# Taps 0 to 3 of a convolution on four 64x64 tiles of TensorE in place of two 64x128 tiles

## The chip, the cores and the metric

The kernel runs on one core of one Trainium2 chip. The metric is the device time of one execution in microseconds (us). Before the change it is 3138.06 us, the median of 3 runs that lie between 3136.07 and 3140.17 us.

## The reference, cut to what matters

Three layers of the same form (layers 0 to 2) and then a fourth of another kind work on `x`, 4 images of 32x32 positions with 16 channels, all in float32. The change touches only the first three:

```python
first = jnp.einsum('ijpq,bpqc->bijc', M2, inputs)
K = jnp.transpose(G, (2, 3, 4, 0, 1, 5)).reshape(kh, kw, c, h * w * f)
shifted = lax.conv_general_dilated(inputs, K, window_strides=(1, 1), padding='SAME',
                                   dimension_numbers=('NHWC', 'HWIO', 'NHWC'))
shifted = shifted.reshape(b, h, w, h, w, f)
diff = jax.nn.relu(inputs[:, :, :, None, None, :] - shifted)
second = jnp.einsum('ijpq,bpqijc->bijc', W2, diff)
return first - L * second
...
x = x + _L0_conv_ref(_gn(x), L0_conv_M, L0_conv_Wp, L0_conv_G)
```

`shifted` is a 3x3 convolution with 1024 x 16 = 16384 output channels: each position (i, j) has filters of its own, and each of them is run over the whole image. `second` then weighs the 1024 image positions for every (i, j) and adds them up. `_gn` is a group norm. The fourth layer is a filter with an infinite impulse response, done in the reference through FFTs; the kernel does it as products with a Toeplitz matrix.

## The kernel before, in words

The 16384 output channels of a layer are cut into 128 blocks of 128 (8 positions by 16 channels). One block for one of the 4 images is called a **group** here; three layers have 3 x 128 x 4 = 1536 groups, and they make up nearly all of the work.

In a group (`conv_layer`, lines 464 to 486) TensorE computes the convolution of the block for all 1024 positions into a PSUM tile `pt` of 128 partitions by 2 by 512. The two `half`s are the upper and lower 16 image rows. Half 0 takes its operands from SBUF partitions 0 to 63 and half 1 from 64 to 127, so that the two are on different row tiles of the array, each 64 rows by 128 columns, and run side by side. Nine taps of 16 channels are 144 rows of contraction, which are split in three steps `n`:

- n = 0: `ga`, taps 0 to 3 of the reordered list (line 41), 64 rows, float32
- n = 1: `gb`, the next four taps, 64 rows, float32
- n = 2: `gn`, the ninth tap, 64 rows in float32r. Its 16 channels stand there four times: the rounded weights and the remainders, against the high and low parts of the image.

A float32 product appears in the trace as two pairs of a weight load (LDWEIGHTS) and a product (MATMUL), a float32r product as one pair. So the 3072 calls with `ga` (1536 groups, two halves) are 6144 records, and the 3072 calls with `gn` are 3072.

`prepare_g` (line 386) subtracts the identity from the centre tap in `ga`, so that `pt` holds `shifted - inputs`. VectorE then does min(pt, 0) times W and adds up along the 1024 positions in one instruction (line 478). Its result is the block's part of `- second`.

The order of the work is written out by hand (`manual_schedule`, line 76). PSUM has 4 buffers `pt`; a group's first product waits until VectorE has read the buffer's last contents. After every group, `step()` advances what stands in `todo`, and after every block one step of `beside` runs. These put other TensorE work between two groups: `first_term` (line 324, 128 rows by 64 columns, two column tiles; line 312, transposes on the whole array), the impulse response in layer 0 (lines 523, 566 and 605, shape 64x128, and for the last, shorter block of line 523 shape 64x64), and group sums (line 101). After the last group, line 761 does the fourth layer on four tiles of 128 rows by 32 columns.

Weights come in by DMA on the SP queue: W for two blocks at a time (`load_w`, line 409, 6 buffers), G for eight blocks at a time (`load_g`, line 364; 2 buffers for `ga`, `gb` and `gn`, and one for the ninth tap's source `g9`). `prepare_g` for the next eight blocks runs in the midst of a chunk, partly on ACT (line 402) and VectorE (line 405).

Of the kernel before, what the change touches and what calls it, by code (L numbers as in the profile page):

```python
# [37 lines left out]
P = 128  # L38
B, C, S = 4, 16, 32
# [4 lines left out]
GC = 8  # L44
# [10 lines left out]
def conv_stack_kernel(ctx, tc, x, raw, w0, M, W, G, den, num, h0, cst, dft, one, idp, idq, out):  # L55
    nc = tc.nc
# [13 lines left out]
    def pair_psum():  # L70
        return ps.tile([P, 2, 512], F32, tag="pt", name="pt")
# [292 lines left out]
    def load_g(layer, ch, parts=((slice(0, GC), nc.sync, nc.sync, nc.sync),)):  # L364

        layer, ch = at = chunk(layer, ch)
        if layer == 3 or at in gr:
            return
        gr[at] = ga, gb, g9 = [
            pool.tile([P, GC, P], F32, tag=tag, name=tag) for pool, tag in ((gs, "ga"), (gs, "gb"), (gp, "g9"))  # L370
        ]
        flat = lambda t: t.rearrange("r n m -> r (n m)")
        for part, *queues in parts:
            src = G[layer][:, (ch * GC + part.start) * P : (ch * GC + part.stop) * P]
            for half in range(2):
                rows = slice(64 * half, 64 * half + 64)
                queues[0].dma_start(out=flat(ga[rows, part]), in_=src[:64])
                queues[1].dma_start(out=flat(gb[rows, part]), in_=src[64:P])
            yield
            queues[2].dma_start(  # L380
                out=flat(g9[:, part]),
                in_=src[P : P + C].unsqueeze(0).to_broadcast([8, C, (part.stop - part.start) * P]),
            )
            yield

    def prepare_g(layer, ch, part=slice(0, GC)):


        at = chunk(layer, ch)
        if at[0] == 3 or (part.start == 0 and at in gt):  # L390
            return
        if part.start == 0:
            gt[at] = *gr[at][:2], gs.tile([P, GC, P], F32R, tag="gn", name="gn")
        ga, gb, gn = (t[:, part] for t in gt[at])
        g9 = gr[at][2][:, part]

        gv = ga.rearrange("r n (p f) -> r (n p) f", f=C)
        nc.gpsimd.tensor_tensor(  # L398
            gv, gv, mid.unsqueeze(1).to_broadcast([P, gv.shape[1], C]), ALU.subtract
        )  # L400
        yield
        nc.scalar.copy(gn, g9)  # L402
        for r in (32, 96):
            lo = gn[r : r + 32]
            nc.vector.tensor_tensor(lo, g9[r : r + 32], lo.bitcast(F32), ALU.subtract)  # L405
# [3 lines left out]
    def load_w():  # L409

        layer, at = divmod(len(wts), NBLK // 2)
        if layer == 3:
            return
        cc, q = divmod(2 * at, S)
        wt = wp.tile([P, 2, S * S], F32, tag="w", name="w")
        src = W[layer][cc, :, q : q + 2, :].rearrange("p k m -> p (k m)")
        nc.sync.dma_start(
            out=wt.rearrange("p k m -> p (k m)"),
            in_=src.unsqueeze(1).to_broadcast([8, C, 2 * S * S]) if wts else w0,
        )  # L420
        wts.append(wt)
# [3 lines left out]
    def step():  # L425
        todo[:] = [t for t in todo if next(t, t) is not t]

    def drain():
        while todo:
            step()  # L430

    def conv_layer(layer, xt, finish, side=(), late=iter(())):


        acc = [work.tile([P, 2, NBLK], F32, tag=f"acc{a}", name=f"acc{a}") for a in range(2)]
        xn = xp.tile([P, B, NBLK], F32, tag="x", name="x")
        result = {}

        def beside():
            result["xr"] = yield from first_term(layer, xt)  # L440
            yield from side

        beside = beside()
        last = range(NBLK - GC, NBLK)

        jobs = [(range(GC), (0, 1)), (range(GC), (2, 3))] if layer else [(range(GC), range(B))]
        jobs += [(range(blk, blk + GC), range(B)) for blk in range(GC, NBLK - GC, GC)]
        jobs += [(last, (0, 1)), (last, (2, 3))]
        for job, (blks, batches) in enumerate(jobs):
            pairs = layer and job < 2, job >= len(jobs) - 2  # L450
            for k, blk in enumerate(blks):
                if any(pairs):

                    if k in ((4, 6) if job != len(jobs) - 2 else (0, 2)):
                        load_w()
                elif k % 2 == 0:
                    load_w()
                if k == (3 if job == 0 else 1):
                    list(load_g(layer, blk // GC + 1))
                if (job or not layer) and k == 6:  # L460
                    list(prepare_g(layer, blk // GC + 1))
                if job == len(jobs) - 2:
                    next(late, None)
                wt = wts[64 * layer + blk // 2][:, blk % 2, :]
                for b in batches:
                    pt = pair_psum()
                    for n, (w, im) in enumerate(zip(gt[layer, blk // GC], ims[b // 2])):
                        for half in range(2):
                            rows = slice(64 * half, 64 * half + 64)
                            nc.tensor.matmul(  # L470
                                pt[:, half, :],
                                lhsT=w[rows, blk % GC, :],
                                rhs=im[rows, :, b % 2, :, :S],
                                start=n == 0,
                                stop=n == 2,
                            )
                    junk = junkp.tile([P, S * S], F32, tag="junk", name="junk")
                    nc.vector.scalar_tensor_tensor(  # L478
                        junk,
                        pt.rearrange("p h m -> p (h m)"),  # L480
                        0.0,
                        wt,
                        ALU.min,
                        ALU.mult,
                        accum_out=acc[b // 2][:, b % 2, blk : blk + 1],
                    )
                    step()
                if not any(pairs) and layer + job:
                    next(beside, None)
            if pairs[1]:  # L490
                a = batches[0] // 2
                two = slice(2 * a, 2 * a + 2)
                nc.vector.tensor_tensor(xn[:, two], result["xr"][:, two], acc[a], ALU.add)  # L493
                drain()
                todo.append(finish(a, xn))
                step()
        return xn
# [151 lines left out]
    with tc.tile_pool(name="st", bufs=1) as st:  # L649
        halves = slice(0, 2), slice(2, GC)  # L650
        load_first(0, 0, nc.sync)
        load_first(0, 1, nc.scalar)
        load_first(0, 2, nc.gpsimd)
        loads = load_g(
            0,
            0,
            (
                (halves[0], nc.sync, nc.scalar, nc.gpsimd),
                (halves[1], nc.sync, nc.sync, nc.gpsimd),
            ),  # L660
        )
        next(loads)
        next(loads)
        load_first(1, 0, nc.sync)
        load_first(1, 1, nc.sync)
        load_first(1, 2, nc.gpsimd)
        load_w()
        list(loads)
        first_images()
        load_w()  # L670
        loads = load_g(0, 1)
        next(loads)
        load_w()
        load_w()
        todo.append(loads)
        xs = conv_layer(0, xs, make_image, impulse_response())
    xs = conv_layer(1, xs, make_image)


# [45 lines left out]
    def late_toeplitz():  # L725
# [7 lines left out]
        yield from load_toeplitz(order[TB + 1], *parts)  # L733

    xs = conv_layer(2, xs, norm3, toeplitz(), late_toeplitz())
    drain()

# [15 lines left out]
    for n, k in enumerate(order):  # L753
        if n == 1:
            list(load_toeplitz(order[-1], toeplitz_tile(tp)))
        for slot in slots[k // 2]:
            for cc in range(4):
                for tile, block, q in slot:
# [5 lines left out]
                        lhsT=y3[:, cc, at : at + 8, :].rearrange("p q b -> p (q b)"),  # L764
                        rhs=ts[n][q][:, :, : S - 8 * cc],
                        start=(tile, block) not in every[:done],
                        stop=(tile, block) not in every[done + 1 :],
# [105 lines left out]
```

## Time and profile before

| what | value |
|---|---|
| median of 3 runs | 3138.06 us |
| the profiled execution, whole | 3145.93 us |
| its span, first to last instruction | 3144.1 us |
| granted TensorE clock, mean | 0.997 |
| first and last end of a group | 16.5 us, 3087.0 us |
| line 470, products with `ga`, `gb`, `gn` | 6144, 6144, 3072 records |
| line 470, loads with `ga`, `gb`, `gn` | 188, 186, 186 ns mean |
| line 478 on VectorE | 1536 of 1225 ns, and 1536 of 83 ns to read the sum |

The profile shows one execution. PE is TensorE's products, PEld its weight loads, which overlap the products; DVE is VectorE, ACT ScalarE, POOL GpSimd, and SP the queue that issues most DMAs. A group line reads: line, engine, operation, output and inputs, shape of the array's part used (rows by columns), operand, count, then busy time and mean of one, then the idle time ahead of it and what ended that. The products are pipelined: a record covers the whole way of a product through the array, and the next one's record begins before it has ended. So the distance from one record's start to the next one's is what a product costs, not its length. The chain of waits follows the work that ended last back to the start, step by step, and shows it in order of time.

### The profile page before, as it was taken

What the parts mean: (1) busy time and instruction counts of PE and PEld (TensorE: products, weight loads), DVE (VectorE), ACT (ScalarE), POOL (GpSimd) and SP (SyncE); (2) the same over time, 40 slices, a digit from 0 to 9 for tenths busy, and PEclk for the clock granted to TensorE, in tenths of its full rate; (3) what the DMA queues carried; (4) which work ended last, traced back from release to release, by engine and by line L of the source; (5) the groups of instructions that cost most, each with busy time, mean ns of one, the idle gap of its engine ahead of it and who ended that gap; (6) DMA issues with size and microseconds to landing.
All of it is one profiled execution on the core that took longest, in us unless ns stands there. A gap on an engine that the chain in (4) does not pass through costs nothing.

```text
span 3144.1 us, 39279 instructions
## 1 busy us (share of the span) xinstructions
PE 3113.4 (99%) x16260; PEld 1538.3 (49%) x16260; DVE 2070.0 (66%) x3318; ACT 81.8 (3%) x107; POOL 232.6 (7%) x258
## 2 busy tenths in 40 slices
PE   7999999999999999999999999999999999999998
PEld 3445554445544554444444444455444444444444
DVE  6666766666666766666666666776666666666662
ACT  1000000000000000000000000000000000000000
POOL 1002321000000100100000000010010000000000
PEclk9999999999999999999999999999999999999999
DMA  7554344433343565433333344265544444444411
GB/s 167 150 125 106 83 105 107 104 91 88 87 103 78 121 141 129 98 88 88 97 98 88 87 97 98 69 133 145 126 106 103 96 106 108 101 97 107 111 31 21
DMA packets 67462, 321.20 MB, mean 102 GB/s; under 512 B 10114, under 2 KB 17028, under 8 KB 41812
## 3 DMA queue, kind: packets, MB, share of 16 engines
q1 hardware_dynamic: 56496, 300.10, 40.5%
q10 hardware_dynamic: 6484, 10.81, 1.7%
q0 software_dynamic: 4304, 7.79, 1.3%
q8 instruction: 127, 2.08, 0.3%
q14 instruction: 51, 0.42, 0.1%
HBM read 313.03 MB, written 5.63 MB: 101 GB/s over the span
## 4 chain that ended last, share of the span: by engine, by line
PE 97%; DMA 2%; DVE 1%; issue 0%; SPq 0%; ACT 0%; DVEq 0%
PE pt L470 94%; PE pt L761 1%; DMA g<-in_G_dram 1%; DMA w<-in_W_dram 1%; PE pt L324 1%; DMA im<-in_raw_dram 0%; DVE junk L478 0%; PE pt L523 0%; PE pt L566 0%; PE pt L605 0%; PE pt L101 0%; DVE x L493 0%; DVE s L110 0%; PE pt L312 0%; DVE gn L405 0%
## 5 line engine op out<-in xcount | busy, mean ns | idle before, releaser
L478 DVE SCALAR_TENSOR_TENSOR junk<-pt,w 128x1024 f32<-128x1024 f32 x1536 | 1881.1, 1225 | 996.8 <-PE pt L470 979.9
L470 PE MATMUL pt<-im,ga 64*128 64x512 f32 x6144 | 1587.1, 591 | 7.5 <-DVE junk L478 4.6
L470 PE MATMUL pt<-im,gb 64*128 64x512 f32 x6144 | 1578.2, 589 | 3.2 <-ACT im L179 3.2
L470 PE MATMUL pt<-im,gn 64*128 64x512 f32 x3072 | 1252.3, 806 | 0.0
L470 PEld LDWEIGHTS pt<-im,gb 64*128 64x128 f32 x6144 | 596.1, 186 | 730.6 <-issue 724.2
L470 PEld LDWEIGHTS pt<-im,ga 64*128 64x128 f32 x6144 | 600.3, 188 | 443.4 <-DVE junk L478 286.4
L470 PEld LDWEIGHTS pt<-im,gn 64*128 64x128 f32 x3072 | 299.8, 186 | 361.8 <-issue 360.6
L398 POOL TENSOR_TENSOR ga<-ga,cs 128x1024 f32<-128x1024 f32 (+2 forms) x49 | 113.5, 2316 | 2131.9 <-DMA ga<-in_G_dram 2131.0
L405 DVE TENSOR_TENSOR gn<-g,gn 32x1024 fp32r<-32x1024 f32 (+2 forms) x98 | 120.7, 1231 | 12.4 <-ACT gn L402 10.2
L478 DVE DVE_READ_ACCUMULATOR junk<-pt,w 128x1 f32 x1536 | 128.0, 83 | 0.0
L402 ACT CAST gn<-g 128x1024 fp32r<-128x1024 f32 (+2 forms) x49 | 50.4, 1028 | 2357.7 <-DMA g<-in_G_dram 2133.7
L348 POOL DMA_DIRECT2D fd<-ft x48 | 25.1, 531 | 229.0 <-DVE ft L341 212.7
L761 PE MATMUL pt<-t,y 128*32 128x128 f32 (+3 forms) x544 | 39.3, 452 | 2.4 <-DVE y L701 2.4
L761 PEld LDWEIGHTS pt<-t,y 128*32 128x32 f32 x544 | 18.3, 114 | 23.1 <-issue 20.5
L774 DVE TENSOR_TENSOR xo<-xo,pt 32x512 f32<-32x512 f32 x5 | 3.4, 682 | 35.9 <-PE pt L761 35.8
L324 PE MATMUL pt<-mt,yt 128*64 128x512 f32 x96 | 21.9, 598 | 0.0
L290 POOL DMA_DIRECT2D im<-img x32 | 16.2, 513 | 9.0 <-DMA img<-y 8.8
L544 POOL TENSOR_TENSOR H<-H,d 128x256 f32<-128x256 f32 (+1 forms) x10 | 8.3, 825 | 68.1 <-DVE d L549 67.8
L324 PEld LDWEIGHTS pt<-mt,yt 128*64 128x64 f32 x96 | 6.4, 136 | 13.7 <-issue 9.7
L101 PE MATMUL pt<-s,cs 64*128 64x2 f32 (+1 forms) x28 | 2.9, 266 | 9.1 <-DVE s L110 9.1
L273 POOL COPY e<-y 32x612 f32<-32x612 f32 x4 | 2.8, 692 | 119.2 <-DVE y L272 119.2
L544 POOL TENSOR_TENSOR t<-s 128x256 f32<-128x256 f32 (+1 forms) x15 | 11.3, 755 | 0.0
(83 smaller groups left out, 192.5 us busy)
## 6 DMA issues: line engine op xcount, KB each, us to landing
w<-in_W_dram SPq DMA_DIRECT2D x191, 1024.0 KB
ga<-in_G_dram SPq DMA_DIRECT2D x94, 256.0 KB
gb<-in_G_dram SPq DMA_DIRECT2D x94, 256.0 KB
g<-in_G_dram SPq DMA_DIRECT2D x47, 512.0 KB
mt<-in_M_dram SPq DMA_DIRECT2D x24, 512.0 KB
t<-hd ACTq DMA_DIRECT2D x28, 160.0 KB
t<-hd SPq DMA_DIRECT2D x28, 160.0 KB
im<-img SPq DMA_DIRECT2D x32, 67.5 KB
```

The lines of the kernel that those rows point to most:

```text
L101: nc.tensor.matmul(pt[:, h, : s.shape[1]], lhsT=avg[rows], rhs=s[rows], start=True, stop=True)
L290: (nc.sync, nc.scalar, nc.gpsimd)[n % 3].dma_start(out=ims[a][k][at : at + C] .bitcast(F32) .rearrange("c l b cc x -> c l (b cc x)")[:, :, ...
L324: nc.tensor.matmul(pf[64 * h : 64 * h + 64], lhsT=yt[:, 4 * part + k].rearrange("k b c -> k (b c)"), rhs=mts[k][:, h, :], start=(k == 0), ...
L348: nc.gpsimd.dma_start(out=fv[h, cc, b], in_=ft[at : at + C, cc])
L398: nc.gpsimd.tensor_tensor(gv, gv, mid.unsqueeze(1).to_broadcast([P, gv.shape[1], C]), ALU.subtract)
L402: nc.scalar.copy(gn, g9)
L405: nc.vector.tensor_tensor(lo, g9[r : r + 32], lo.bitcast(F32), ALU.subtract)
L470: nc.tensor.matmul(pt[:, half, :], lhsT=w[rows, blk % GC, :], rhs=im[rows, :, b % 2, :, :S], start=n == 0, stop=n == 2,)
L478: nc.vector.scalar_tensor_tensor(junk, pt.rearrange("p h m -> p (h m)"), 0.0, wt, ALU.min, ALU.mult, accum_out=acc[b // 2][:, b % 2, blk : ...
L544: mul = lambda o, u, w: nc.gpsimd.tensor_tensor(o, u, w, ALU.mult)
L761: nc.tensor.matmul(bank[32 * tile : 32 * tile + 32] .rearrange("n (j r) -> n j r", j=C)[:, :, 8 * cc :], lhsT=y3[:, cc, at : at + 8, :].re ...
L774: nc.vector.tensor_tensor(row, row, src, ALU.add)
```

## The change

The products with `ga` (n = 0) are split by output column: each call of 64 rows by 128 columns becomes two calls of 64 rows by 64 columns, of which one writes partitions 0 to 63 of `pt` and the other 64 to 127. With the two halves these are the four 64x64 tiles of the array. `gb` and `gn` stay on two 64x128 tiles. The arithmetic, the operands in SBUF and everything on the other engines stay as they are.

```diff
                     for n, (w, im) in enumerate(zip(gt[layer, blk // GC], ims[b // 2])):
                         for half in range(2):
                             rows = slice(64 * half, 64 * half + 64)
-                            nc.tensor.matmul(
-                                pt[:, half, :],
-                                lhsT=w[rows, blk % GC, :],
-                                rhs=im[rows, :, b % 2, :, :S],
-                                start=n == 0,
-                                stop=n == 2,
-                            )
+
+                            for c in (slice(0, 64), slice(64, P)) if n == 0 else (slice(0, P),):
+                                nc.tensor.matmul(
+                                    pt[c, half, :],
+                                    lhsT=w[rows, blk % GC, c],
+                                    rhs=im[rows, :, b % 2, :, :S],
+                                    start=n == 0,
+                                    stop=n == 2,
+                                )
```

## The prediction

> **What bounds the kernel now.** I read the page's busy line and chain first, then the groups by line, then the chain of waits in order of time, and last the loads one by one in two short stretches. The first extract is from the page.
>
> ```profile
> PE 3113.4 (99%) x16260; PEld 1538.3 (49%) x16260; DVE 2070.0 (66%) x3318; ACT 81.8 (3%) x107; POOL 232.6 (7%) x258
> ...
> PE pt L470 94%; PE pt L761 1%; DMA g<-in_G_dram 1%; DMA w<-in_W_dram 1%; PE pt L324 1%; DMA im<-in_raw_dram 0%; DVE junk L478 0%; PE pt L523 0%; PE pt L566 0%; PE pt L605 0%; PE pt L101 0%; DVE x L493 0%; DVE s L110 0%; PE pt L312 0%; DVE gn L405 0%
> ...
> L478 DVE SCALAR_TENSOR_TENSOR junk<-pt,w 128x1024 f32<-128x1024 f32 x1536 | 1881.1, 1225 | 996.8 <-PE pt L470 979.9
> L470 PE MATMUL pt<-im,ga 64*128 64x512 f32 x6144 | 1587.1, 591 | 7.5 <-DVE junk L478 4.6
> L470 PE MATMUL pt<-im,gb 64*128 64x512 f32 x6144 | 1578.2, 589 | 3.2 <-ACT im L179 3.2
> L470 PE MATMUL pt<-im,gn 64*128 64x512 f32 x3072 | 1252.3, 806 | 0.0
> ```
>
> TensorE is the bound: line 470 is 94% of the chain, and VectorE's reduction (line 478) stood idle 979.9 us waiting for it. 1536 groups (one block and one batch each) run. The records of line 470 overlap, so their means (591, 589, 806 ns) are latencies and not costs. The cost is the step between starts. In the steady stretch around 1502 us these are, per half of the rows, with the other half running beside it: first to second ga pass pair 434 ns, ga to gb 429, gb to gb 428, gb to gn 429 (the single-pass gn has its start hidden in its record, so I take the start of its stream as one step after the second gb), gn to the next ga 243. The sum is 1.963 us, which is also the median distance of the ends of successive groups over the whole run. Only two terms hold anything but streaming: 434 against 429, and 243 against the 216 ns that one pass takes (half of a 429 pair, and the step of line 523's 256-column pairs). So **27 + 5 = 32 ns a group** is all that better-hidden weight loads could return, 49 us in 1536 groups.
>
> That stall is where the change aims: the ga load starts when the gn stream starts, takes 186 ns, and the ga stream starts 57 ns after it ends.
>
> ```profile
> 1501.22 0.19 PEld L470 LDWEIGHTS pt<-im,gn 64*128 64x128 f32 x2 [0.24 <-issue]
> 1501.24 0.81 PE L470 MATMUL pt<-im,gn 64*128 64x512 f32 x2
> 1501.65 0.44 PEld L470 LDWEIGHTS pt<-im,ga 64*128 64x128 f32 x4 [0.24 <-DVE junk L478]
> 1501.89 1.03 PE L470 MATMUL pt<-im,ga 64*128 64x512 f32 x4
> ```
>
> Now the place that decides. The kernel already runs a few products of another shape between two groups: line 523 does five blocks of eight, four of shape 64x128 and the last of 64x64. First this last one, load by load (columns: start, duration, engine, what):
>
> ```profile
> 384.07 0.20 PEld L470 LDWEIGHTS pt<-im,gn 64*128 64x128 f32 x2 [0.23 <-issue]
> 384.10 0.82 PE L470 MATMUL pt<-im,gn 64*128 64x512 f32 x2
> ...
> 384.85 0.63 PEld L523 LDWEIGHTS pt<-ab,table 64*64 64x64 f32 x8 [0.57 <-DVE junk L478]
> 384.85 1.08 PE L523 MATMUL pt<-ab,table 64*64 64x256 f32 x8
> ...
> 385.86 0.30 PEld L470 LDWEIGHTS pt<-im,ga 64*128 64x128 f32 x4 [0.39 <-issue]
> ```
>
> Then the chain in order of time over three of the blocks (start, length, what):
>
> ```profile
> 336.09 0.86 PE pt L523 x8
> 336.96 23.55 PE pt L470 x120
> 360.51 0.86 PE pt L523 x8
> 361.37 23.55 PE pt L470 x120
> 384.92 1.01 PE pt L523 x8
> 385.94 23.76 PE pt L470 x120
> 409.69 0.86 PE pt L566 x8
> ```
>
> The reader is to see that a next load normally starts 0.43 us after the gn load (1501.22 to 1501.65), but 0.78 us after it when the shape goes from 64x128 to 64x64 (384.07 to 384.85): it stays out until the gn stream, ending at 384.72, has left the array. The named releaser, line 478, cannot be the cause: the 64x128 blocks of line 523 wait on the same semaphore, and their load at 360.09 comes 0.43 us after the gn load. In the chain, block and twelve groups take 0.86 + 23.55 = 24.41 us where the shape stays and 1.01 + 23.76 = 24.77 where it goes to 64x64 and back, with the same streaming. **A round trip costs 0.35 to 0.36 us** (0.351 by the one group period that holds it).
>
> **What the Trainium skill says.** "TensorEngine Tiling (Array Packing)", Key Properties: going to another tiling mode, not merely to another tile, drains TensorE. The trace agrees, with the 0.35 us above. "TensorE: Matmul & The Clock Gate", LDWEIGHTS: the time of a load goes by its columns, at 1.2 per ns, thus 107 ns for 128 and 53 for 64. The trace agrees in the difference: the records take 186 ns and 129 to 133 ns. The same page, The mechanism: loads overlap running products only on other row groups. The trace disagrees: the gb load at 1500.361 starts beside a ga product on its own rows, which then streams for 429 ns.
>
> **The change, part by part.**
> (1) Instructions. The ga calls go from 3072 to 6144, so their records from 6144 to 12288; gb and gn keep theirs. A group has 28 records (14 loads, 14 products) in place of 20. Line 761 issues 640 products and as many loads in 45.64 us, 28 records per us; 28 in 2.33 us is 12 per us. Issue is no limit.
> (2) Streaming of ga. Four 64x64 tiles at once, each two pass pairs, should take the 858 ns that two 64x128 tiles take. No row shows four such tiles. The nearest are line 324, where two column halves of all 128 rows run 16 products in 3.58 us (16/2 x 0.429 = 3.43 and a change of shape), and line 761 with four column tiles side by side (steps of 322 ns for pairs of 384 columns, 320 by streaming). From below it costs 0; from above, if two tiles on the same rows take turns, 858 ns a group. I take 0.
> (3) The removed stall: the 32 ns would go only if the ga load ran under gn. By (4) it does not; nothing is credited.
> (4) Changes of shape. gn is 64x128, ga now 64x64, gb 64x128 again: a round trip in every group. Split by the stream starts around line 523: into 64x64, 384.502 to 384.904, 402 ns where 243 stood, so +159; out of it, the stream ends at 385.765 and the next starts at 385.970, +205 where nothing stood. Together 364 less the few ns that the first ga pair takes extra now, again 0.35 to 0.36; I take 0.355. Line 324 gives the same: from 161.89 to 228.50 us there are 66.61 us, less 32 x 1.963 and 3.43, leaves 0.36. A third, line 312 with 128x128, gives 0.35. From below: nothing, if such a change costs only what a 64x64 block showed by chance; three shapes agreeing excludes it as far as two active tiles can. The gap cannot hide: the products on both sides need TensorE itself.
> (5) Four tiles in place of two at each change: loads are issued about 7 ns apart (384.852, 384.859), so the last tile starts 14 ns later than now, and its end decides when gb may load. I take 10 ns; from below 0; from above, if the loads of one row half take turns, another 53 to 57 ns (one 64-column load), or 160 if all four did.
> Sum: 0.355 + 0.010 = **0.365 us a group**, period 2.328 us, 1536 x 0.365 = +560.6 us.
> (6) What hides some. Group 28 ends at 74.94 us and the next 6.9 us late: the g block issued at 39.57 lands at 74.7 (chain: 35.14 us), VectorE's queue stands behind it at line 405. Slower groups arrive some 8 us later there, but part of that comes back, as W buffers and so transfers are freed later. I take -5, bounds 0 and -10. Places that change shape already (six of line 324, three of line 312, one of line 523) gain one change and not two: about -0.15 each, -1.5 in all.
> (7) VectorE has 1.31 us of work (1225 + 83 ns) in 2.33 us; its wait grows and nothing waits for it. DMA, SP and POOL issue nothing more; W and G loads get more time. No semaphore wait is added: behind the stalled loads in TensorE's queue stand only products of the same group, and line 478 waits longer for them. The part after the last group, from 3087 us, holds no ga.
> Total: 560.6 - 5 - 1.5 = +554 us on the profiled execution's 3145.93 us (span 3144.1), 3700 us. That execution stands 0.25% above the median of the three runs; 3138.06 x 3700/3145.93 = **3691 us**, 18% slower.
>
> **Rivals.**
> A, faster: the drain is not paid, since all tiles sit on the same rows and the array's background weights take the 64-column loads. Then the 133 ns load and 57 ns after it, 190, fit under 216 of gn, and up to 32 ns a group go: 1536 x 0.032 = 49, **3089 us**. For it speaks the shorter load; against it all ten round trips in the trace, each with a full stop. Break-even is where a round trip costs 32 ns, a tenth of what it shows. Chance 6%, of which 1% falls within 0.2% of before.
> B, much slower: two tiles on the same 64 rows take turns, since they read the same image rows: +858 ns a group more, 1318 us, **about 5010 us**. Lines 324 and 761 speak against it; that four 64x64 tiles are in no row speaks for it. 6%.
> C: loads of four tiles take turns after each drain, +53 to 160 ns a group: 80 to 245 us more, 3770 to 3940 us. 10%.
> Forecast: 78%.
>
> **How the numbers follow.** The forecast's own bounds: 0.346 us a group and 10 hidden give 531 - 11.5, 3657 us; 0.42 (one load in turn) and nothing hidden give 645, 3780 us. To take in the lower edge of a drain partly hidden (0.33) and most of C's near half: 3630 to 3800. Left out are A, B and the far half of C, under 2 in 10. About 0.2%, 6 us, is what a measurement tells from no change: faster 0.05, same 0.01, slower 0.94.
>
> **What would show each step.** Right: group period 2.31 to 2.35 us; the first ga load about 0.78 us after the gn load instead of 0.43; the first gb load starting about 0.1 us after the last ga stream has ended, not beside it; ga loads of about 130 ns, 12288 of them; ga's second pair still 429 ns after the first; VectorE waiting some 550 us more. Wrong: a gn-to-ga step near 216 ns (A), ga pairs 858 ns apart (B), or the four first ga loads of a group spread over more than 30 ns (C).

## The result and the profile after

The changed kernel takes 3681.7 us (median of 4 runs, 3681.15 to 3683.01) where the kernel before takes 3139.11 us, run beside it: a ratio of 1.1728, 95% interval 1.1707 to 1.1748. It is slower by 542.6 us. The profiled execution took 3681.21 us, its span 3679.4 us.

The page of the changed kernel, the lines that answer to those shown of before (line 470 is now 472, 478 is 480):

```profile
PE 3655.1 (99%) x22404; PEld 1121.7 (30%) x22404; DVE 2067.2 (56%) x3318; ACT 81.8 (2%) x107; POOL 232.6 (6%) x258
...
L480 DVE SCALAR_TENSOR_TENSOR junk<-pt,w 128x1024 f32<-128x1024 f32 x1536 | 1879.9, 1224 | 1541.9 <-PE pt L472 1527.7
L472 PE MATMUL pt<-im,gb 64*128 64x512 f32 x6144 | 1735.0, 641 | 2.5 <-ACT im L179 2.5
L472 PE MATMUL pt<-im,ga 64*64 64x512 f32 x12288 | 1674.6, 615 | 3.2 <-POOL ga L398 3.2
L472 PE MATMUL pt<-im,gn 64*128 64x512 f32 x3072 | 1246.3, 804 | 0.0
```

PE is busy 99% here as it was before; that share does not show the loss. Two other things do: VectorE waits 1527.7 us for line 472 where it waited 979.9, and the weight loads' busy time, which counts stretches in which any load is under way, fell from 1538.3 to 1121.7 us although the loads are more in number (22404 for 16260). The 64-column loads are short, as meant (131 ns in the mean where the 128-column ones took 188), and no time is saved by it.

One group of the changed kernel in order of time (start, duration, engine, what):

```profile
1501.54 0.19 PEld L472 LDWEIGHTS pt<-im,gn 64*128 64x128 f32 x2 [0.24 <-issue]
1501.57 0.81 PE L472 MATMUL pt<-im,gn 64*128 64x512 f32 x2
1502.31 0.21 PEld L472 LDWEIGHTS pt<-im,ga 64*64 64x64 f32 x8 [0.58 <-issue]
1502.31 1.09 PE L472 MATMUL pt<-im,ga 64*64 64x512 f32 x8
...
1503.33 0.30 PEld L472 LDWEIGHTS pt<-im,gb 64*128 64x128 f32 x4 [0.81 <-issue]
1503.33 1.13 PE L472 MATMUL pt<-im,gb 64*128 64x512 f32 x4
...
1503.87 0.19 PEld L472 LDWEIGHTS pt<-im,gn 64*128 64x128 f32 x2 [0.24 <-issue]
```

The ga load comes 0.77 us after the gn load; before, it came 0.43 us after. The gb load and the gb product's record begin together, 0.8 us after the last ga load has ended: nothing of the gb load lies beside ga's streams any more. The next gn load comes 0.54 us after that. Of this, 0.11 us lie between the first gb load and the second, which starts when the first one's product begins to stream; the other 0.43 us are the usual step.

The chain of the changed kernel in order of time, over the same blocks of the impulse response (line 525 now):

```profile
380.45 0.86 PE pt L525 x8
381.31 27.86 PE pt L472 x166
409.18 0.86 PE pt L525 x8
410.04 27.86 PE pt L472 x166
437.90 0.79 PE pt L525 x5
438.69 0.22 PE pt L472 x2
438.90 0.01 PE pt L525
438.91 27.70 PE pt L472 x164
466.62 0.86 PE pt L568 x8
```

Block and twelve groups take 28.73 us (380.45 to 409.18) where they took 24.41 before: 0.36 us a group. The last block, of shape 64x64, costs nothing extra now (437.90 to 466.62 is 28.72 us), since ga, which follows it, has its shape.

### The profile page after: what moved, and what is told of

Its sections match the earlier page's. It is cut to its first block, busy times and chain, and to the rows that moved or that the text cites. A ratio compares the mean times of both kernels' runs of the same rounds, so it can differ in the third digit from the quotient of the medians.

```text
span 3679.4 us, 51567 instructions
## 1 busy us (share of the span) xinstructions
PE 3655.1 (99%) x22404; PEld 1121.7 (30%) x22404; DVE 2067.2 (56%) x3318; ACT 81.8 (2%) x107; POOL 232.6 (6%) x258
## 4 chain that ended last, share of the span: by engine, by line
PE 99%; DMA 1%; DVE 0%; ACT 0%; POOL 0%; issue 0%; POOLq 0%
PE pt L472 97%; PE pt L763 1%; PE pt L324 1%; DMA im<-in_raw_dram 0%; PE pt L568 0%; PE pt L525 0%; DMA x<-in_x_dram 0%; PE pt L607 0%; PE pt L101 0%; DVE junk L480 0%; PE pt L312 0%; POOL im L193 0%; ACT im L175 0%; DVE sq L124 0%; DVE xc L119 0%
## 5 line engine op out<-in xcount | busy, mean ns | idle before, releaser
L480 DVE SCALAR_TENSOR_TENSOR junk<-pt,w 128x1024 f32<-128x1024 f32 x1536 | 1879.9, 1224 | 1541.9 <-PE pt L472 1527.7
L472 PE MATMUL pt<-im,gb 64*128 64x512 f32 x6144 | 1735.0, 641 | 2.5 <-ACT im L179 2.5
L472 PE MATMUL pt<-im,ga 64*64 64x512 f32 x12288 | 1674.6, 615 | 3.2 <-POOL ga L398 3.2
L472 PEld LDWEIGHTS pt<-im,gb 64*128 64x128 f32 x6144 | 462.6, 184 | 1250.6 <-issue 1245.5
L472 PEld LDWEIGHTS pt<-im,ga 64*64 64x64 f32 x12288 | 319.5, 131 | 874.9 <-issue 834.5
```

The lines of the kernel that those rows point to most:

```text
L472: nc.tensor.matmul(pt[c, half, :], lhsT=w[rows, blk % GC, c], rhs=im[rows, :, b % 2, :, :S], start=n == 0, stop=n == 2,)
L480: nc.vector.scalar_tensor_tensor(junk, pt.rearrange("p h m -> p (h m)"), 0.0, wt, ALU.min, ALU.mult, accum_out=acc[b // 2][:, b % 2, blk : ...
```

## The experiments

The theory: at each change between 64x128 and 64x64 TensorE first finishes what it is streaming (it drains) and only then loads the next weights; one round trip, there and back, is 0.36 us. The rival: the 64x64 tiles cost the time themselves, by their doubled loads and products. Times below are medians; periods are the mean distance of line 478's starts over 360 groups in the middle of the run, 1.9633 us before and 2.3217 us after the change.

**1. gb on 64x64 tiles too.**

```diff
-for c in (slice(0, 64), slice(64, P)) if n == 0 else (slice(0, P),):
+for c in (slice(0, 64), slice(64, P)) if n < 2 else (slice(0, P),):
```

> gb goes on four 64x64 tiles as well as ga; gn stays on two 64x128 tiles. Theory (each change of the array's shape costs a drain): still one round trip in a group, now between gb and gn and between gn and ga. Group period 2.32 us, about 3680 us, as with ga alone; ga to gb steps 429 ns. Rival (the 64x64 tiles themselves cost, by their number of loads or products): twice the cost, 1.963 + 2 x 0.361 = 2.685 us a group, about 4230 us.

Measured: 3682.95 us, ratio to before 1.1733 (1.1714 to 1.1753); period 2.3217 us. Twice as many 64x64 products cost nothing more. The stop moved: ga to gb is a plain 429 ns step, and gb to gn now holds it. The rival in this form falls. The weight loads of a group in order of time, up to the next gn:

```profile
1501.68 0.21 PEld L474 LDWEIGHTS pt<-im,ga 64*64 64x64 f32 x8 [0.26 <-issue]
1502.17 0.15 PEld L474 LDWEIGHTS pt<-im,gb 64*64 64x64 f32 x4 [0.28 <-issue]
1502.60 0.15 PEld L474 LDWEIGHTS pt<-im,gb 64*64 64x64 f32 x4 [0.28 <-issue]
1503.56 0.19 PEld L474 LDWEIGHTS pt<-im,gn 64*128 64x128 f32 x2 [0.81 <-issue]
```

**2. Every second group backwards.** The same 64x64 products as in the change, with half the changes of shape.

```diff
-for n, (w, im) in enumerate(...):
+order = (0, 1, 2) if b % 2 == 0 else (2, 1, 0)
+for at, n in enumerate(order):
...
-start=n == 0, stop=n == 2,
+start=at == 0, stop=at == 2,
```

> ga alone on 64x64 tiles as in the change, but every second group runs its steps backwards (gn, gb, ga), so that gn meets gn and ga meets ga. Theory: one change of shape in a group in place of two, half of 0.361, period about 2.14 us in the mean; 1536 x 0.18 = 277 less some 10 absorbed at the start, about 3405 us. Rival (64x64 tiles cost by themselves): as many of them as before, about 3680 us.

Measured: 3415.15 us, ratio 1.0879 (1.0863 to 1.0895); period 2.1433 us, which is 0.1800 above before against 0.3584 for the change: half. The 10 us that were expected to be absorbed at the start were not (1536 x 0.18 is 276.5 us, and 276.6 were measured). The weight loads of this kernel in order of time:

```profile
1500.78 0.21 PEld L474 LDWEIGHTS pt<-im,ga 64*64 64x64 f32 x8 [0.76 <-issue]
1501.26 0.15 PEld L474 LDWEIGHTS pt<-im,ga 64*64 64x64 f32 x4 [0.28 <-DVE junk L482]
1501.69 0.15 PEld L474 LDWEIGHTS pt<-im,ga 64*64 64x64 f32 x4 [0.28 <-issue]
1502.65 0.30 PEld L474 LDWEIGHTS pt<-im,gb 64*128 64x128 f32 x4 [0.81 <-issue]
1503.19 0.19 PEld L474 LDWEIGHTS pt<-im,gn 64*128 64x128 f32 x2 [0.24 <-issue]
1503.62 0.19 PEld L474 LDWEIGHTS pt<-im,gn 64*128 64x128 f32 x2 [0.23 <-issue]
```

Between two groups ga follows ga, and loads come 0.48 and 0.43 us apart with 0.28 us of idle; only entering ga (0.76 idle) and leaving it (0.81) is there a stop.

**3 and 4. A whole kernel in either shape.** gn's operands are taken as float32, so that all three steps may have one shape; no run has a float32r gn on 64x64 tiles.

```diff
+if n == 2:
+    w, im = w.bitcast(F32), im.bitcast(F32)
...
-for c in (slice(0, 64), slice(64, P)) if n == 0 else (slice(0, P),):
+for c in (slice(0, P),):                        # run 3
+for c in (slice(0, 64), slice(64, P)):          # run 4
```

> The partner of the next run: gn's operands are taken as float32, all three steps on 64x128 tiles. Both theories: three double pass pairs of 429 ns for each row half, period 6 x 0.429 = 2.574 us, 1536 x 0.611 = 938 less some 15 absorbed at the start, about 4060 us; the 27 ns after gn gone, since a load has 429 ns of cover.

> gn's operands as float32 and all three steps on four 64x64 tiles: twice the instructions and no change of shape between or within groups. Theory: the same as its partner on 64x128 tiles, period 2.574 us, about 4060 us, within 10 us. Rival (64x64 tiles cost by themselves): 3 x 0.361 more, period 3.66 us, about 5730 us; with a cost only where ga stands, 2.935 us and about 4615 us.

Measured: 4072.46 us (run 3) and 4079.48 us (run 4), both with a period of 2.575 us. Twice the loads and products in the steady state: no difference. (Run 3 lies 12 us above its expectation, mostly because only some 6 us were absorbed at the start, not 15.) The 7 us between them have a place. The chain in order of time, run 3 first:

```profile
450.49 0.86 PE pt L530 x8
451.35 30.90 PE pt L477 x144
482.25 1.01 PE pt L530 x8
483.26 31.10 PE pt L477 x144
514.36 0.86 PE pt L573 x8
```

and run 4:

```profile
419.39 1.06 PE pt L530 x8
420.45 31.06 PE pt L477 x288
451.51 1.06 PE pt L530 x8
452.58 31.06 PE pt L477 x288
483.64 0.63 PE pt L530 x5
484.26 0.21 PE pt L477 x2
484.48 0.01 PE pt L530
484.49 30.90 PE pt L477 x286
515.39 1.06 PE pt L573 x8
```

This is one picture and its mirror image. Where the groups are 64x128, the 64x64 block costs 0.35 us (482.25 to 514.36 is 32.11 us, the block before it 31.76). Where the groups are 64x64, the 64x128 blocks cost 0.37 us (419.39 to 451.51, 32.12 us) and the 64x64 block is free (31.75). The same instructions pay or do not pay by their neighbours alone. This shows the theory. Summed up group by group, the impulse response in layer 0 makes run 4 4.7 us longer than run 3, and the group sums at the ends of layers 1.7 us; the part after the last group takes 1.2 us back. The profiled executions differ by 4.75 us, the medians by 7.0.

**5, 6, 7. What the 27 ns after gn are.** The change meant to hide ga's load under the single pass of gn. Would that have paid without the stop? S1: the 128-column load is too long for one pass. S2: the stall belongs to float32r. Run 5 has run 2's order with all steps on 64x128 tiles; run 6 reads gn's operands as bfloat16, and run 7 does so on 64x64 tiles throughout.

```diff
+w, im = w.bitcast(BF16)[:, :, 1::2], im.bitcast(BF16)[:, :, :, :, 1::2]   # n == 2, runs 6 and 7
```

> The kernel before with every second group's steps run backwards (gn, gb, ga), all on 64x128 tiles. On the 27 ns between gn and the next load's product. S1 (the load of 128 columns does not fit under one pass): gn to gn and gn to gb each 243 ns, the sum as before, 3138 us within 5. S2 (the 27 ns belong to the step from float32r to float32, not to the load): gn to gn is 216 ns, one stall for two groups, 1536 x 0.0135 = 21 us less, about 3117 us.

> gn's operands are read as bfloat16 (the upper halves of the same words), so the ninth tap is computed in lower precision; all on 64x128 tiles. The partner of the next run. S1 (load of 128 columns too long for one pass): gn to ga stays 243 ns, period 1.963, 3138 us. S2 (a matter of the float32r type): 216 ns, period 1.931 to 1.936 us, about 3092 us.

> gn's operands read as bfloat16 (ninth tap in lower precision), all three steps on four 64x64 tiles: single-pass gn beside 64-column loads without a change of shape. S1: the load fits under one pass, gn to ga 216 ns, period 1.931 us, about 3089 us, 49 us below before, what the change would have given without the drain. S2: no better than its partner on 64x128 tiles. If the 64x64 tiles cost by themselves: 2.3 us or more, above 3680 us.

Measured: 3134.68 us (ratio 0.9988, 0.9980 to 0.9997), 3130.84 us (0.9976, 0.9968 to 0.9984) and 3139.23 us (1.0000, 0.9992 to 1.0008), in the order of the runs. The steps: gn to gn 241 ns and gn to gb 243 in run 5; gn to ga 240 in run 6 and 239 in run 7. Runs 5 and 6 are against S2: the stall stays where gn follows gn, and where gn is not float32r. They are near what S1 had expected, and run 7 is against S1. Both theories fall. Run 7 has what the change was after, 64-column loads (134 ns) beside a single pass with no change of shape, and gains nothing. It is even 8 us slower than its partner run 6: its period is 2.8 ns longer (1.9611 against 1.9583 us), about 4 us in all, for a cause that stays open, and the rest fits the other shapes' blocks, as between runs 3 and 4. Products of run 7 in order of time:

```profile
1500.40 0.41 PE L477 MATMUL pt<-im,gn 64*64 64x512 bf16 x4
1500.64 1.03 PE L477 MATMUL pt<-im,ga 64*64 64x512 f32 x8
```

The shorter load is done well before; the pass itself takes 239 ns. New theories: A1, the operand's short rows (16 runs of 32 words with gaps between them) slow the single pass; A2, the 4-byte step between its values does; B, each single pass pays a fixed price.

**8 to 11. The pass alone.** Run 8 reads longer rows of the same tile (the ninth tap then sees shifted data); runs 9 and 10 read 512 contiguous 2-byte values of a constant table in its place, with gn's weights read as in run 6 (the ninth tap is left out), on 64x128 and on 64x64 tiles; run 11 splits gn in two halves. Runs 8 and 11 have 64x128 tiles throughout.

```diff
+rhs=im[rows, :, b % 2].rearrange("r l cc x -> r l (cc x)")[:, :, :128]   # run 8, n == 2
+rhs=cs.bitcast(BF16)[rows, :512]                                         # runs 9 and 10, n == 2
+for part in (slice(0, 2), slice(2, 4)):                                  # run 11, n == 2
+    nc.tensor.matmul(pt[:, half, 128 * part.start : 128 * part.stop], ..., rhs=im[rows, part, b % 2, :, :S])
```

> The kernel before, with gn's image operand read in 4 runs of 128 words in place of 16 runs of 32 with gaps (other positions, so the ninth tap is computed from shifted data). On the 24 to 27 ns that the single pass takes beyond 216. A1 (reading short rows limits the pass): gn to ga 216 ns, period 1.936, about 3097 us. A2 (the width of the words limits it) and B (a fixed price of a single pass): no change, 1.963 us, 3138 us.

> gn's image operand replaced by 512 contiguous bfloat16 values of a constant table, its weights read as bfloat16: the ninth tap is left out and a product of the same shape stands in its place; all on 64x128 tiles. A1 and A2 (reading limits the pass): gn to ga 216 ns, period 1.934 us, about 3092 us. B (a fixed price of a single pass): as with bfloat16 at a 4-byte step, 1.958 us, 3131 us.

> The same operand (ninth tap left out), all three steps on four 64x64 tiles. Whether the length of the weight load counts for anything once the operand's reading is cheap: if 64 columns help, below its partner on 64x128 tiles by up to 24 ns a group, 37 us; if not, the same within 10 us.

> gn's product split in two of 256 columns each, same data and weights, all on 64x128 tiles. A1 and A2: the excess goes with the columns, the two together 243 ns[...]; 3138 to 3175 us. B: each pass pays 24 to 27 ns, period 1.99 us, about 3178 us. If a load beside a short pass needs its whole 186 to 215 ns, each half takes 215: period 2.15, about 3425 us.

Measured: run 8 3119.19 us (0.9934, 0.9917 to 0.9951), period 1.950; run 9 3093.97 us (0.9856, 0.9842 to 0.9871), period 1.9325; run 10 3097.87 us (0.9870, 0.9855 to 0.9885), period 1.9325; run 11 3143.49 us (1.0017, 1.0008 to 1.0025), period 1.9667. The products of run 9 in order of time:

```profile
1500.30 0.38 PE L477 MATMUL pt<-cs,gn 64*128 64x512 bf16 x2
1500.52 1.02 PE L477 MATMUL pt<-im,ga 64*128 64x512 f32 x4
```

The gn pass takes 215 ns, with the same 128-column load for ga (187 ns) beside it. B falls by run 11 (two passes cost 3 ns more than one, not 25) and by run 9. S1 is answered once more by runs 9 and 10, which have the same period (their medians are 4 us apart, in the same direction as those of runs 3 and 4): load length counts for nothing. What is left is the form in which the image is read. A1 has a part: longer rows alone give 13 ns a group (run 8), not the 27 that A1 had expected. Contiguous 2-byte values give 31 ns (run 9), which leaves a part for A2; but run 9 also read another tile with other data, so that this part is argued and not shown. Run 8 also changed the data; run 12 below has long rows with the true data.

**12. The ninth tap's image without gaps.** All of the reference is computed. The image tile of gn is stored as 512 words in a row per image; it has to be loaded at the layer changes in shorter pieces. All is on 64x128 tiles. The code that loads, fills and clears this tile changes too and is not shown.

```diff
-imp.tile([P, 4, 2, 4, 34], d, ...)
+imp.tile([P, 4, 2, 4, 34] if k < 2 else [P, 2, 4, 4, S], d, ...)
...
-rhs=im[rows, :, b % 2, :, :S],
+rhs=im[rows, :, b % 2, :, :S] if n < 2 else im[rows, b % 2],
```

> The kernel before, computing all that the reference asks for, with the ninth tap's image tile stored without gaps (per image 512 words in a row in place of 16 rows of 32 words 34 apart), all on 64x128 tiles. If the reading of the image is the stall: at least what 4 runs of 128 words gave, period 1.950 us or less, about 3119 us, and at best the 1.9325 us of the 2-byte operand, about 3095 us; at the layer changes 56 more and shorter image loads for each image pair, on three queues, which have some 31 us of cover each and so should cost nothing. If the gain of the runs before came from other data and not from the reading order: 3138 us.

Measured: 3131.33 us, ratio 0.9974 (0.9961 to 0.9986), period 1.9467 us. This is faster than both kernels, than the one before by 0.26%, which is small but clear of its interval. In the steady state it gains what was expected, 16.6 ns x 1536 = 25 us. The other part of the expectation was wrong: the loads are not covered. The chain in order of time at the first layer change:

```profile
1021.46 5.05 DMA im<-img
1026.52 0.28 issue
1026.80 0.51 POOL im L297
1027.31 0.12 issue
1027.43 3.99 POOL im L297 x8
...
1036.81 3.52 POOL im L297 x7
1040.33 8.12 DMA im<-img
1048.45 1.66 issue
1050.11 4.26 PE pt L484 x10
```

The small DMAs are issued one after another at 0.5 us each on the POOL queue, and the last lands at 1048 us. Counted from 0, group 513 ends 6.1 us later than its period and group 514 another 1.5 us (before: 0.9 us for the two together), and the next layer change repeats it: against before, 8 to 9 us are lost at each of the two changes. A packed layout that is loaded in larger pieces was not tried.

## Why the prediction was right

3691 us were predicted, 3681.7 measured, 9 us less; the profiled execution was put at 3700 us and took 3681.2. The mechanism was the one forecast: each group pays for two changes of shape. Of the 19 us by which the sum for the profiled execution was too high, 10 are the drain and nearly 9 the cover.

- **The drain (step 4)**, 0.355 us a group with its 10 ns for four tiles (step 5), predicted 0.365: measured 0.358 in the mean. A first product's record after a change begins with its load; its stream begins when the second load does. By these starts, in the group shown: into 64x64, 395 ns where 243 stood (+152, predicted +159); out of it, 644 ns from the second ga pair to gb where 429 stood (+215, predicted +205 and the tiles' 10); less the 5 ns of the first ga pair. 0.0066 us x 1536 is the 10 us.
- **What the skill says** of it ("TensorEngine Tiling (Array Packing)", Key Properties: a change of mode drains, a change of tile does not) is borne out by runs 1 to 4: four tiles, of one shape, cost nothing.
- **Streaming and issue (steps 1 and 2)**: 12288 records of ga; the second pairs follow 429 ns after the first pairs' streams; no turns between tiles. Rival B is out. The four first ga loads of a group spread over 20 ns (1502.311 to 1502.331): rival C is out.
- **The cover (step 6)** was put at -6.5 us in all. Between the profiled executions it was 15. The first 36 groups gave back 10 us, since the stall after group 28 was gone entirely. But this stall comes and goes with the execution: the profiled ones of before and of runs 6, 8 and 9 have it, those of runs 5, 7, 10, 11 and 12, with nearly the same periods, do not, and the profiled execution of before lay 8 us above its median. The other shapes' places gave back 5 us where 1.5 had been put: line 324 0.2 each (0.15 predicted), and the group sums 2.8 in all, which the prediction left out. So the medians differ by 542.6 us and the profiled executions by 535.3. Between the medians, 1536 x 0.3584 is 550.5, and about 8 us came back. That this is near 6.5 is in part luck: the stall counted for less than was put, the other places for more.
- **Rival A and the 32 ns (steps 3 and first part)**: no credit was given, because of the drain, and that was right. But the prediction took the 27 ns after gn for a weight load that does not fit under one pass, and that was wrong: runs 7, 9 and 10 show that the load's length had nothing to do with it. Without any drain the change would have given nothing, not 49 us, as far as run 7's bfloat16 gn stands for the float32r one.

## What to carry to other kernels

Before a product is put on smaller tiles, look at its neighbours: if they keep another shape, the change pays two stops of TensorE each time, here 0.36 us together on a 1.96 us group, although the tiles themselves cost nothing. A few odd products that are already in the trace can price this before anything is built: compare the blocks that share the neighbours' shape with the one that does not. And a stall next to a weight load need not be the load's: vary the load and the operand that is streamed separately before building on it.

## What the runs showed of the hardware that was not expected

- A single pass over 512 columns takes 215 ns with contiguous 2-byte values (runs 9 and 10), which agrees with the gap that the Trainium skill, "TensorE: Matmul & The Clock Gate", Back-to-back issue gap, gives for a product by itself (518 cycles at 2.4 GHz for 512 columns, which is 216 ns). With the same count of columns it takes about 230 ns for 4-byte words in a row (run 12), 234 in runs of 128 words (run 8), 240 for 2-byte values at a 4-byte step in runs of 32 (run 6), and 243 for 4-byte words in runs of 32 (before). The section's formula holds the count of columns and the clock alone. Double passes over image rows of the same form, 429 ns, show no such excess.
- By which path the read slows the pass is open. That it is the reading of SBUF is argued from these figures and was not shown by itself; the width of the values, their step and their data were not varied one at a time.
- The cost of a change of shape is the same, 0.35 to 0.36 us a round trip, for 64x64, 128x64 and 128x128 blocks between 64x128 ones (the kernel before). For 64x64 and 64x128, runs 3 and 4 show that it moves to whichever shape is the odd one.
